# A four-part graph, state-space and expert kernel: the third layernorm's moments moved from VectorE to ScalarE, and the planner's due times replaced

## The chip, the cores and the metric

The kernel runs on one core of one Trainium2 chip. A core has five engines that run their own instruction queues in order and wait for each other by semaphores: TensorE (PE, matrix products; its weight loads are listed as PEld), VectorE (DVE), ScalarE (ACT), GpSimd (POOL) and SyncE (SP, which here issues DMAs only). PE writes its results to PSUM, of which the kernel uses eight banks of 512 floats a partition; DVE and ACT read them from there. The metric is the device time of one execution in microseconds (us), median of several runs.

## The reference

The input is x of 64 graphs x 256 nodes x 256 features and an integer adjacency of 64 x 256 x 256. Two layers are applied, each a graph part and a feed-forward part on a layernorm of x, each added to x:

```python
x = x + _L0_gnn_ref(_layernorm(x), adj, W, a)          # attention over the neighbours
x = x + _L0_ffn_ref(_layernorm(x), W_in, conv_w, ...)  # a state-space (Mamba-2) block, one chunk of 256
x = x + _L1_gnn_ref(_layernorm(x), adj, weight, bias)  # relation products: sum over r of (adj == r) @ x @ weight[r]
x = x + _L1_ffn_ref(_layernorm(x), gate_w, w1, w2, ...) # a mixture of 8 experts, one for each token
```

The layernorm has no weights: `(x - mean) / sqrt(var + eps)`. The third one, before the relation products, is the one whose moments the change concerns.

## The kernel before

There are two passes. The first goes through the 16,384 tokens in 32 groups of two graphs (512 rows, four tiles of 128 rows, indexed j). It does everything up to the choice of the expert, and writes x and the list of the experts' tokens to DRAM. The second (L1187 and after) goes through blocks of tokens of one expert; it gathers rows, does both products and scatters the result. The change is in the first pass only.

A group passes four functions, which add steps to a plan. (Matrix products go through the helper `product`, so the profile gives nearly all of them line 585, and tells them apart by their tiles; the lines below are those of the calls.)

- `attention` (L641): loads x (tile `x`, five buffers) and the adjacency (`adji`), makes the mask `hide`; transposes x to `xT`; takes the first layernorm's moments; products with `wx` to `wh`; attention scores `ev` (three operations over 1024 columns on DVE, L698 to L702, then the exponentials, L705), transposed to `eT`; the attention products `wh,eT` (L728), added to x (L731).
- `scan` (L736): the second layernorm, `xn` and its transpose `xnT`; the step sizes `dt` by a row of some fifteen small DVE operations (L755 to L772); nine input projections `xnT,win` (L777), four of them gates (`gate`) and five convolved: ACT writes `y` (L797), DVE adds three taps (L804), ACT takes the tanh (L810), DVE multiplies (L814, `xh` and `bm`); the decays: PE spreads sums over heads (`sel`, L865), ACT makes `dm` by 32 small relus (L871) and four exponentials (L877).
- `mix` (L893): `bc` from `bm` and `cm`; `xdt` (transposes of `xh`, L914, times `dt`, L919); DVE multiplies each `dm` by `bc` (L929); the products `dm,xdt` (L936, L940); the skip term (L946), the gate (`yg`, L949), the squares (L951), added up on POOL (L954, L956); the out-projection `wf,gate` (L985), the row sums (L992), the factor `r2` and its power on POOL (L996, L998), and the update of x (L1001).
- `relate` (L1006): the third layernorm, split into `xhi` (ACT, through `scaled`, L637) and `xlo` (DVE, L1013); the bias added to x by a POOL DMA with addition (`biased`, L632); the relation products with `adjT` (L1031), `hr` (L1038), the products with `wrel` (L1043), the update of x (L1047); the two DMAs of x to DRAM; and the squares for the router's layernorm (`spreads`, L607), which takes the mean that x carries as column 264 of its row.

The moments of the first three layernorms come from `deviations` (L587): four `bn_stats` and four `bn_aggr` on DVE (L601, L604), one addition (L591), and the power -1/2 on POOL (L593). After every second group `choose` (L1060) finds the expert of 1024 tokens and scatters their slots by eight POOL DMAs (L1123).

The order is not that of the code. `Plan.step` notes each step with its engine, a cost in us, and what it reads and writes; `Plan.record` (L175) then emits all steps by a list schedule over the planner's own costs: of the steps of an engine that are ready it takes the one that can begin first, and of those within 0.05 us of each other the one of the lowest rank. A tile of a tag is made only when its buffers are free and the earlier tiles of that tag have been made. The rank is

```python
step = Step(engine, us, go, self.g, self.TAIL[engine] + late, PACE * self.g + DUE[self.k])
```

with g the group and k the step's number within its group, so `DUE` says how much earlier or later than its group a kind of step is due.

Of the kernel before, what the change touches and what calls it, by code (L numbers as in the profile page):

```python
# [14 lines left out]
ALU = mybir.AluOpType  # L15
# [4 lines left out]
P = 128  # L20
# [5 lines left out]
PE, ACT, DVE, POOL, SP = range(5)  # L26
# [1 line left out]

PACE = 21.50
DUE = [
    -273, -768, -7, 206, -128, -104, -233, 716, 257, 96, 325, 660, -290, -837, -1156, -195, -739,
    -864, 633, -563, -1270, 205, -488, -744, -1044, 252, -389, 419, -601, -43, 36, 132, 68, -155,
    389, 355, -223, -943, 4, 450, -281, 40, -502, 21, 982, 124, 113, 525, -49, 159, 104, 239, 309,
    -615, -359, -749, 426, 428, -391, -391, -326, -1237, -329, -546, -645, -815, -544, -187, -763,
    -683, -372, -601, -139, 290, -500, 172, -270, -586, 121, -388, 994, 458, -317, 125, 17, 277,
    17, 326, -210, -907, 100, -221, -383, -517, 6, 127, 610, 247, -329, -914, -875, -432, -1394,
    67, -309, 571, -93, -248, 110, 916, -78, 172, 34, 14, -122, 417, 67, 66, -569, 10, -1389, 19,
    -452, -183, -558, -20, 528, -605, -550, 387, -39, -686, -315, -111, -118, 33, 835, -632, -115,  # L40
    -192, 1375, -454, -252, 210, 224, 52, -419, -132, 69, 455, 629, 386, -646, 24, 58, 481, -861,
    -1548, -751, -773, 201, 9, 281, -95, 348, 383, 19, -696, -531, -135, -484, -660, 65, 182,
    -280, -194, -875, -1264, -1144, 84, 670, 265, 650, 324, 204, 363, 495, 947, 472, -54, 73, 119,
    -1092, -1060, -382, -668, -147, -96, -599, 715, 36, 69, -120, 106, -707, 33, 160, -559, 353,
    178, -313, 230, -326, -579, 295, 367, -2, -489, -468, -22, 96, -289, 98, -712, -377, 214, 73,
    287, -118, 62, -460, -77, -43, -515, 382, 530, -30, 249, 105, -328, 750, 213, -1302, -231,
    579, -503, -197, -40, 69, -338, -470, -134, -1067, -1028, -435, -550, -387, 677, -404, -211,
    -622, -957, -146, -304, 889, -297, 255, 165, 661, -161, -83, 166, -447, -657, -588, -282,
    -1432, -622, 134, -1056, -541, 582, -9, -25, 592, -45, 94, 540, 638, -1240, -75,
]  # L50


# [16 lines left out]
class AtOnce:  # L69
# [20 lines left out]
    def step(self, engine, us, go, reads, writes, late=0.0):  # L90
        go()
# [9 lines left out]
class Plan:  # L101
# [32 lines left out]
    def step(self, engine, us, go, reads, writes, late=0.0):  # L134
        step = Step(engine, us, go, self.g, self.TAIL[engine] + late, PACE * self.g + DUE[self.k])
        self.k += 1
# [117 lines left out]
def gnn_mamba_rgcn_moe(ctx: ExitStack, tc: tile.TileContext, a: dict, out: bass.AP):  # L254
# [10 lines left out]
    nc = tc.nc  # L265
    x, adj = a["x"], a["adj"]
    B, N, D = x.shape
# [16 lines left out]
    EPS = 1e-5  # L284
# [33 lines left out]
    mhalf = const.tile([P, 8], F32, name="mhalf")  # L318
# [263 lines left out]
    def product(out_, pairs):  # L582

        for i, (lhsT, rhs) in enumerate(pairs):
            nc.tensor.matmul(out_, lhsT=lhsT, rhs=rhs, start=(i == 0), stop=(i == len(pairs) - 1))  # L585

    def deviations(s, src, of):  # L587

        mv, ve, rs = s.tile("mv" + of, [P, 4, 2]), s.tile("ve" + of, [P, 4]), s.tile("rs" + of, [P, 4])
        moments(s, src, mv, 0, of)  # L590
        s.step(DVE, 0.07, lambda: nc.vector.tensor_scalar(  # L591
            ve(), mv()[:, :, 1], EPS, None, ALU.add), [mv], [ve])
        s.step(POOL, 1.0, lambda: nc.gpsimd.tensor_tensor(  # L593
            rs(), ve(), mhalf[:, 0:4], ALU.pow), [ve], [rs])
        return ve, rs

    def moments(s, src, mv, o, of):

        sb = s.tile("st" + of, [P, 4, 6])
        for j in range(4):  # L600
            s.step(DVE, 0.34, lambda j=j: nc.vector.bn_stats(sb()[:, j, :], src()[:, j, 0:D]),  # L601
                   [(src, j)], [(sb, j)])
        for j in range(4):
            s.step(DVE, 0.07, lambda j=j: nc.vector.bn_aggr(mv()[:, o + j, :], sb()[:, j, :]),  # L604
                   [(sb, j)], [(mv, o + j)])

    def spreads(s, src, vr, o):  # L607

        left = s.tile("left", [P, D], BF16)
        for j in range(4):  # L610
            s.step(ACT, 0.58, lambda j=j: nc.scalar.activation(
                left(), src()[:, j, 0:D], AF.Square, bias=src()[:, j, DG - 1 : DG],
                accum_out=vr()[:, o + j : o + j + 1]), [(src, j)], [left, (vr, o + j)])
# [16 lines left out]
    def biased(s, xe, bias):  # L630

        s.step(POOL, 1.4, lambda: nc.gpsimd.dma_start(  # L632
            out=xe()[:, :, 0:DG], in_=bias.unsqueeze(1).to_broadcast([P, 4, DG]),
            accum_op=ALU.add), [], [xe], late=4.5)

    def scaled(s, j, dst, src, rs):
        s.step(ACT, 0.4, lambda: nc.scalar.activation(  # L637
            dst()[:, j, :], src()[:, j, 0:D], AF.Copy, scale=rs()[:, j : j + 1]),
            [(src, j), rs], [(dst, j)])
# [365 lines left out]

    def relate(s, js, o, full, xe, adjT, pair):  # L1006

        ve, rs = deviations(s, xe, "3")

        xhi, xlo = s.tile("xhi", [P, 4, D], F32R), s.tile("xlo", [P, 4, D], F32R)  # L1010
        for j in range(4):
            scaled(s, j, xhi, xe, rs)
            s.step(DVE, 0.4, lambda j=j: nc.vector.scalar_tensor_tensor(  # L1013
                xlo()[:, j, :], xe()[:, j, 0:D], rs()[:, j : j + 1], xhi()[:, j, :].bitcast(F32),
                ALU.mult, ALU.subtract), [(xe, j), rs, (xhi, j)], [(xlo, j)])
        biased(s, xe, brel)
        rels = R if full else 1
        for bi in range(2):
            sums = []
            for r in range(rels):  # L1020
                rel = adjT[bi]
                if full:
                    rel = s.tile("rel", [P, 512], F32R)
                    s.step(DVE, 0.45, lambda r=r, bi=bi, rel=rel: nc.vector.tensor_scalar(
                        rel(), adjT[bi]().bitcast(F32), float(r + 1), None, ALU.is_equal),
                        [adjT[bi]], [rel])
                ps, hr = s.psum(), s.tile("hr", [P, 512], bufs=R if full else 2)

                def related(bi=bi, rel=rel, ps=ps):
                    for d in range(2):  # L1030
                        product(ps()[:, d * N : (d + 1) * N], [  # L1031
                            (part()[:, 2 * bi + k, d * P : (d + 1) * P],
                             rel()[:, k * N : (k + 1) * N])
                            for k in range(2) for part in (xhi, xlo)])

                s.step(PE, 1.05, related, [rel, *((p_, 2 * bi + k) for k in range(2)
                                                  for p_ in (xhi, xlo))], [ps])
                s.step(ACT, 0.47, lambda ps=ps, hr=hr: nc.scalar.copy(hr(), ps()), [ps], [hr])  # L1038
                sums.append(hr)
            weights = pair.get("wrel", wrel)  # L1040
            for h in range(2):
                ps, j = s.psum(), 2 * bi + h
                s.step(PE, 0.9, lambda h=h, ps=ps, sums=sums, weights=weights: product(  # L1043
                    ps()[:, :DG], [
                        (sums[r]()[:, d * N + h * P : d * N + (h + 1) * P], weights[:, r, d, :])
                        for r in range(rels) for d in range(2)]), [*sums], [ps])
                s.step(DVE, 0.35, lambda j=j, ps=ps: nc.vector.tensor_add(  # L1047
                    xe()[:, j, 0:DG], ps()[:, :DG], xe()[:, j, 0:DG]), [ps], [(xe, j)])
        for view in (x3v, outv):
            s.step(SP, 0.1, lambda view=view: nc.sync.dma_start(  # L1050
                out=view[:, js, :], in_=xe()[:, :, 0:D]), [xe], [], late=4.5)

        if o == 0:
            pair["vr"], pair["lg"] = s.tile("vr", [P, 8]), s.tile("lg", [P, 8, E + 1])
        lg = pair["lg"]
        s.step(ACT, 0.22, lambda: nc.scalar.copy(lg()[:, o : o + 4, :], xe()[:, :, D:DG]),
               [xe], [(lg, o)])
        spreads(s, xe, pair["vr"], o)
# [70 lines left out]
    def group(s, g, js, pair, toks, full=False):  # L1129


        s.of(g)
        xe, hide, entries = attention(s, g, js, full)
        ahead = scan(s, g, xe)
        adjT = mix(s, xe, entries, full, *ahead)
        relate(s, js, 4 * (g % 2), full, xe, adjT, pair)
        if g % 2:
            s.of(g + 1, first=False)
            choose(s, toks, pair)
# [244 lines left out]
```

## Time and profile before

| what | value |
|---|---|
| median of 3 runs | 2520.09 us (2518.72 to 2521.66) |
| the profiled execution | 2517.28 us, its span 2515.3 us |
| busy: PE, DVE, ACT, POOL | 2393.0, 1921.1, 1641.2, 838.2 us |
| first matmul of the `dm,xdt` products, group 0 and group 31 | 136.2 and 1762.35 us |
| last `wrel` products of the first pass | from 1796.57 us |
| the chain that ended last reaches back to | 1903.33 us, in the second pass |

The profile lists busy time, which is the union of an engine's instructions; since instructions overlap the start of the next one, a mean duration is longer than the distance between two starts. A row of groups has the line, engine, operation, tiles out and in, shapes and count, then total busy time and mean duration in ns, then the engine's idle time just before them and what ended it. A row of waits reads: who waited, for whom, us in total, times, longest. The chain that ended last lies wholly in the second pass in this profile, so the first pass has to be read by stretches of time and by waits.

### The profile page before, as it was taken

The page shows a single profiled execution, that of the slowest core. Times are in us where ns is not written, and L with a number is a line of the kernel's source. Part 1 is how long each engine was busy: PE and PEld are TensorE (multiplying, and loading weights), DVE is VectorE, ACT ScalarE, POOL GpSimd, SP SyncE. Part 2 cuts the span into 40 slices and gives each one's busy share as a digit, 9 for nine tenths or more (in the row PEclk, how much of TensorE's full clock was granted, in tenths as well). Part 3 has the DMA queues.
Part 4 walks back from the last instruction along what each step waited for, and adds up shares of the span by engine and source line. Part 5 has one row for each costly group of instructions (what it writes and reads, how often), then busy time and mean ns, then how long its engine had stood idle before and what let it go on. Part 6 is the DMA issues. An engine that isn't in the chain of part 4 may idle for free. (4 is left out here: it accounts for less than half of the span.)

```text
span 2515.3 us, 35051 instructions
## 1 busy us (share of the span) xinstructions
PE 2393.0 (95%) x11536; PEld 1667.4 (66%) x11536; DVE 1921.1 (76%) x4776; ACT 1641.2 (65%) x3712; POOL 838.2 (33%) x756
## 2 busy tenths in 40 slices
PE   6799999999999999999999999999559999999998
PEld 4566667766677776777766777666446666666665
DVE  3699999999999999999999999999623344334443
ACT  0688788888888888888888888888312222332232
POOL 0122343343333433334343343432532222222222
PEclk7899999999999999999999999999779999999999
DMA  2302222223222232222332222312264333333333
GB/s 79 100 12 64 63 54 62 64 67 75 54 62 54 71 79 56 54 62 70 68 67 53 62 68 57 81 37 54 52 194 122 122 107 116 120 115 117 110 124 74
DMA packets 171135, 196.53 MB, mean 78 GB/s; under 512 B 24919, under 2 KB 155807, under 8 KB 170800
## 3 DMA queue, kind: packets, MB, share of 16 engines
q1 hardware_dynamic: 122144, 133.11, 16.9%
q0 software_dynamic: 47104, 59.14, 12.7%
q8 instruction: 97, 1.59, 0.3%
q10 hardware_dynamic: 1680, 1.79, 0.2%
q14 instruction: 110, 0.90, 0.1%
HBM read 109.05 MB, written 47.06 MB: 62 GB/s over the span
## 5 line engine op out<-in xcount | busy, mean ns | idle before, releaser
L585 PE MATMUL ps<-xnT,win 128*128 128x512 f32 x1152 | 546.1, 600 | 3.9 <-ACT xnT L627 3.9
L804 DVE SCALAR_TENSOR_TENSOR y<-ps,cw,y 128x510 f32<-128x510 f32 (+2 forms) x480 | 349.6, 738 | 6.1 <-ACT y L797 2.8
L871 ACT ACTIVATE dm<-ps,cs 128x256 f32<-128x256 f32 (+1 forms) x1024 | 334.1, 475 | 11.5 <-PE ps L585 11.4
L593 POOL TENSOR_TENSOR rs<-ve,mhalf 128x4 f32<-128x4 f32 x96 | 155.1, 1616 | 508.2 <-DVE ve L591 490.3
L1298 PE MATMUL ps<-xnT,w 128*128 128x512 f32 (+1 forms) x768 | 318.0, 573 | 3.9 <-DVEq L1346 3.9
L1308 PE MATMUL ps<-w,hid 128*128 128x256 f32 x1440 | 318.7, 379 | 0.0
L585 PEld LDWEIGHTS ps<-xnT,win 128*128 128x128 f32 x1152 | 203.1, 190 | 166.1 <-issue 153.7
L1308 PEld LDWEIGHTS ps<-w,hid 128*128 128x128 f32 x1440 | 271.7, 190 | 44.9 <-issue 10.0
L1298 PEld LDWEIGHTS ps<-xnT,w 128*128 128x128 f32 x768 | 148.1, 193 | 161.2 <-issue 147.9
L585 PE MATMUL ps<-wf,gate 128*128 128x265 f32 x1024 | 251.9, 389 | 1.0 <-DVE gate L949 0.6
L1302 ACT ACTIVATE hid<-ps,b 128x512 f32<-128x512 f32 (+1 forms) x192 | 126.8, 661 | 183.1 <-PE ps L1298 183.1
L1313 DVE TENSOR_TENSOR yv<-ps,b 128x256 f32<-128x256 f32 x90 | 38.2, 425 | 254.4 <-PE ps L1308 254.4
L585 PEld LDWEIGHTS ps<-wf,gate 128*128 128x128 f32 x1024 | 192.8, 191 | 49.4 <-issue 11.3
L929 DVE TENSOR_TENSOR dm<-dm,bc 128x1536 f32<-128x1536 f32 x128 | 224.1, 1754 | 0.8 <-ACT dm L877 0.2
L1329 POOL DMA_INDIRECT out_dram<-yf,place x90 | 89.1, 990 | 372.3 <-DVE yf L1328 366.9
L877 ACT ACTIVATE dm<-dm 128x1536 f32<-128x1536 f32 x128 | 198.9, 1558 | 0.0
L1123 POOL DMA_INDIRECT slots<-meta,sl x128 | 133.5, 1043 | 191.0 <-DVE sl L1120 150.8
L1314 ACT ACTIVATE yv<-yv,meta 128x256 f32<-128x256 f32 x90 | 45.8, 508 | 201.5 <-DVE yv L1313 201.5
L936 PE MATMUL ps<-dm,xdt 128*64 128x256 f32 x1024 | 168.6, 396 | 4.7 <-DVE dm L929 4.4
L601 DVE BATCH_NORM_STATS2 st<-x 128x6 f32<-128x256 f32 x384 | 155.1, 416 | 6.1 <-DMA x<-in_x_dram 4.5
L954 POOL TENSOR_TENSOR xh<-xh 128x512 f32<-128x512 f32 x64 | 107.5, 1680 | 132.2 <-ACT xh L951 132.1
L585 PE MATMUL ps<-wh,eT 128*128 128x273 f32 x512 | 143.5, 405 | 0.0
(244 smaller groups left out, 4913.3 us busy)
## 6 DMA issues: line engine op xcount, KB each, us to landing
w<-in_L_ffn_w_dram SPq DMA_DIRECT2D x52, 1024.0 KB, 5.6
x<-blin POOLq DMA_DIRECT2D x32, 530.0 KB, 7.3
x<-brel POOLq DMA_DIRECT2D x32, 530.0 KB, 7.0
adji<-in_adj_dram SPq DMA_DIRECT2D x32, 512.0 KB, 3.9
x<-in_x_dram SPq DMA_DIRECT2D x32, 512.0 KB, 4.9
x3d<-x SPq DMA_DIRECT2D x32, 512.0 KB, 3.1
out_dram<-x SPq DMA_DIRECT2D x32, 512.0 KB, 4.1
cm<-bm SPq DMA_DIRECT2D x32, 128.0 KB, 2.2
```

The lines of the kernel that those rows point to most:

```text
L585: nc.tensor.matmul(out_, lhsT=lhsT, rhs=rhs, start=(i == 0), stop=(i == len(pairs) - 1))
L593: s.step(POOL, 1.0, lambda: nc.gpsimd.tensor_tensor(rs(), ve(), mhalf[:, 0:4], ALU.pow), [ve], [rs])
L601: s.step(DVE, 0.34, lambda j=j: nc.vector.bn_stats(sb()[:, j, :], src()[:, j, 0:D]), [(src, j)], [(sb, j)])
L804: nc.vector.scalar_tensor_tensor(y3[:, :, d:], p3[:, :, : N - d], cw[:, c, k : k + 1], y3[:, :, d:], ALU.mult, ALU.add,)
L871: nc.scalar.activation(dm()[:, q, bi, o : o + n], ps()[:, t0 + N - n : t0 + N], AF.Relu, bias=cs()[:, j, h : h + 1], scale=-1.0,)
L877: s.step(ACT, 1.38, lambda: nc.scalar.activation(dm(), dm(), AF.Exp, scale=-1.0), [], [dm])
L929: s.step(DVE, 1.67, lambda dm=dm: nc.vector.tensor_mul(dm(), dm(), bc().unsqueeze(1).to_broadcast([P, 2, 2, N + P])), [bc], [dm])
L936: nc.tensor.matmul(o, lhsT=xdt()[:, 2 * bi, h * 64 : (h + 1) * 64], rhs=dm()[:, q, bi, 0:N], start=True, stop=False,)
L1123: s.step(POOL, 1.1, lambda j=j: apart("slots", nc.gpsimd.indirect_dma_start(out=slots, out_offset=bass.IndirectOffsetOnAxis(ap=sl()[:, j : ...
L1298: nc.tensor.matmul(ps[:, :n], lhsT=w1[:, k, f * P : (f + 1) * P], rhs=xnT[:, k, :], start=(k == 0), stop=(k == 1),)
L1302: nc.scalar.activation(hid[:, f, :], ps[:, :n], AF.Relu, bias=self.b1[i % 2][:, f : f + 1])
L1308: nc.tensor.matmul(ps[:, :D], lhsT=hid[:, f, j * P : (j + 1) * P], rhs=w2[:, f, :], start=(f == 0), stop=(f == NFT - 1),)
```

## The change

Two things change. In `relate` the third layernorm's moments no longer come from `deviations`; four ACT squares take the deviations from the mean in x's row and sum them (`spreads`, with the same single buffer `left` as the router's squares), DVE turns the sums into variance plus eps, POOL takes the power. And the table of due times is replaced: all of the offsets become 0, and `PACE` becomes 13.60. The list has a number for each step of a group, in the order in which the functions add them.

```diff
-PACE = 21.50
+PACE = 13.60
 DUE = [
-    -273, -768, -7, 206, -128, -104, -233, 716, 257, 96, 325, 660, -290, -837, -1156, -195, -739,
...
-    -1432, -622, 134, -1056, -541, 582, -9, -25, 592, -45, 94, 540, 638, -1240, -75,
+    0, 0, 0, 0, 0, 0, 0, 0, 0, 0, 0, 0, 0, 0, 0, 0, 0, 0, 0, 0, 0, 0, 0, 0, 0, 0, 0, 0, 0, 0, 0,
...
 ]
@@
     def relate(s, js, o, full, xe, adjT, pair):
 
-        ve, rs = deviations(s, xe, "3")
+        vr, rs = s.tile("vr3", [P, 4]), s.tile("rs3", [P, 4])
+        spreads(s, xe, vr, 0)
+        s.step(DVE, 0.07, lambda: nc.vector.tensor_scalar(
+            vr(), vr(), 1.0 / D, EPS, ALU.mult, ALU.add), [], [vr])
+        s.step(POOL, 1.0, lambda: nc.gpsimd.tensor_tensor(
+            rs(), vr(), mhalf[:, 0:4], ALU.pow), [vr], [rs])
```

## The prediction

> **What bounds the kernel now.** I read the page first, then the busy time by stretches, then the waits of single engines, then rows by shape. The page:
>
> ```profile
> span 2515.3 us, 35051 instructions
> ...
> PE   6799999999999999999999999999559999999998
> ...
> DVE  3699999999999999999999999999623344334443
> ACT  0688788888888888888888888888312222332232
> ```
>
> Slices 3 to 28 are the first pass (32 groups of four 128-row tiles), the rest is the experts' pass. The change touches the first pass alone; the experts' pass I leave at its time. The first pass by stretches (columns: PE, weight loads, DVE, ACT, POOL busy, granted clock, DMA):
>
> ```profile
> 125.00:600.00 475.00, 469.64 (x2495) 329.16 (x2494) 451.16 (x1024) 402.62 (x942) 161.36 (x133) 1.00 0.25 55
> 600.00:1100.00 500.00, 497.42 (x2665) 349.47 (x2664) 477.21 (x1135) 426.04 (x1000) 197.48 (x164) 1.00 0.29 66
> 1100.00:1700.00 600.00, 595.97 (x3164) 419.02 (x3163) 572.71 (x1362) 504.96 (x1184) 229.65 (x189) 1.00 0.27 61
> ```
>
> PE is busy 1563 of 1575 us, 99.2%, at full clock; DVE 95.3%, ACT 84.7%. The busy PE really streams: in the timeline the projections' matmuls follow each other every 0.43 us. PE waits, from 125 to 1700 us:
>
> ```profile
> PE ps L585 <- ACT xnT L627: 3.4, 15, 0.2
> PE ps L622 <- ACT xn L637: 3.1, 15, 0.2
> ```
>
> So PE sets the pace, and only 12 us of the pass are left to win. The first `dm,xdt` matmul of group 0 starts at 136.2 us, that of the last group at 1762.35: 1626 us for 31 steps, 52.5 us a group. Work a group: PE 52, DVE 50, ACT 44.5. All three are near full, so the order in which they are fed decides.
>
> **Part 1, the third layernorm's moments.** The rows:
>
> ```profile
> L593 POOL TENSOR_TENSOR rs<-ve,mhalf 128x4 f32<-128x4 f32 x96 | 155.1, 1616 | 508.2 <-DVE ve L591 490.3 <-DVE mv L604 11.6 <-ACT wh L675 6.1
> L601 DVE BATCH_NORM_STATS2 st<-x 128x6 f32<-128x256 f32 x384 | 155.1, 416 | 6.1 <-DMA x<-in_x_dram 4.5
> ...
> L604 DVE BATCH_NORM_AGGREGATE mv<-st 128x2 f32<-128x6 f32 x384 | 65.1, 173 | 1.6
> ```
>
> Four of each leave DVE per group. Durations overlap the next start, so I use the distance of starts: 0.33 and 0.09 us. 4 x 0.42 = 1.7 us, over 32 groups 54 us of DVE. The small `ve` operation and the POOL power (1.6 us) stay, one for one. ACT gets four squares with the sum read out; the router's four squares are the same shape. At the end of the pass they stand back to back:
>
> ```profile
> 1805.59 0.51 ACT L611 ACTIVATE left<-x 128x256 bf16<-128x256 f32 x1
> 1806.01 0.19 ACT L611 ACTIVATION_READ_ACCUMULATOR left<-x 128x1 f32 x1
> 1806.22 0.51 ACT L611 ACTIVATE left<-x 128x256 bf16<-128x256 f32 x1
> ```
>
> 0.63 us from start to start, 2.5 us a group, 80 us of ACT in all: DVE 48, ACT 47 a group, both under PE's 52. If PE stayed covered, this part would be worth nothing, with all of PE's idle time (12 us) as the most it could give. Two orders are new: both uses of squares share one `left` buffer, so group g+1's moments stand behind group g's router squares; and on ACT they stand ahead of `xhi`. Neither matters at 52 us a group: from the first of the moments' squares to x complete it is some 16 us in the walk below. The small DVE operation on the variance now waits for ACT's squares; behind it on DVE stand the next group's x updates, its statistics and `xlo`, for which POOL's power and PE's relation products wait.
>
> **Part 2, the due times.** All offsets become 0, so of steps that could start together the older group's goes first, whatever PACE is. I read the order of the changed program's instructions on each engine. It repeats every two groups from group 2 to 27. Counting PE's own work (its instructions by their distances in the trace) from a group's first `dm,xdt` matmul: before, its last `wrel` product comes 101 us later, two groups on, and the next group's attention products stand 15 us ahead of it. After, `wrel` ends 28 to 31 us behind it, and the next group's attention stands 14 us behind it for an even group, 4 us ahead for an odd one. Group g is nearly finished before g+1 may begin its input projections. What hid the latency between engines before (other groups' work) is gone. I walk one even and one odd group through the new order, with starts' distances from the trace (us: convolution tap 0.66, `dm` product 1.68, `x` updates 0.34 to 0.41, ACT copies 0.48, one PE projection 1.71) and about 0.25 us from PE to a reader, 0.1 elsewhere.
>
> Even group g, from its first `dm,xdt` matmul. `dm,xdt` 5.2. DVE's four `yg` are done at 7.8, so PE's out-projection (16 matmuls, 7.2) ends at 13.8, the row sums at 14.6. `r2` and the power (1.2): 16.3. The four L1001 updates: 18.0. PE does g+1's attention only now, 15.9 to 19.6; DVE's updates and stats for it end at 21.7. POOL: third layernorm's power to 21.7, the next group's second to 23.4. ACT: squares 16.9 to 19.7, `xhi` to 23.5, `xn` to 25.1. PE: relation products, half of g+1's transposes, `wrel` to 30.3, other half 30.7. The bias DMA is issued at `xlo`'s end, 24.0, and takes 7.0 (its row): x is complete at 32.5. On ACT the first router square stands ahead of the second `xnT` copy, so this waits for x: 32.7. Only here g+1's projections run. From here to the last `dm` exponential ACT has 29.2 us of own work (32 relus at 0.305 = 9.8, 4 exponentials 5.5, 5 `y` 3.3, 5 tanh 2.7, 4 gates 2.0, `ev` and `exp` 3.0, the rest 2.9) and waits 4.2 for taps and projections: 66.1. The ACT distances are from rows like
>
> ```profile
> 1015.55 5.10 ACT L871 ACTIVATE dm<-ps,cs 128x256 f32<-128x256 f32 x16 [0.68 <-PE ps L585]
> 1020.43 1.60 ACT L877 ACTIVATE dm<-dm 128x1536 f32<-128x1536 f32 x1
> ```
>
> Then the `dm` products and the last `xdt`: the next group's first `dm,xdt` matmul at 70.7.
>
> Odd group. Attention of g+1 is done, `rs` of its second layernorm at 11.5, `xn` at 13.2; but its transposes stand behind the out-projection (8.3 to 15.5) and row sums: 17.2; `xnT` 18.0. L1001 updates done at 19.6, squares at 21.9; the power waits on POOL behind another group's `wh` product and power until 24.0; `xhi` 25.7, `xlo` 26.2, bias lands 33.3, x complete 34.8. ACT from 18.0: 34.5 of own work, 8.3 of waits (1.5 for that power, 2.8 for x, the rest taps): 60.8. Next first `dm,xdt` matmul: 62.9.
>
> **The clock.** While PE idles in front of the `xh` transposes (10 us and more in both walks) its clock falls. The end of the pass shows it (here the clock is the last column but two):
>
> ```profile
> 1766.00:1770.00 4.00, 1.88 (x20) 1.46 (x16) 4.00 (x5) 2.34 (x4) 1.21 (x2) 1.00 0.00 0
> 1770.00:1772.00 2.00, 1.26 (x8) 0.90 (x9) 2.00 (x5) 0.00 (x0) 1.02 (x1) 0.50 0.00 0
> ...
> 1776.00:1778.00 2.00, 2.00 (x9) 1.61 (x8) 2.00 (x8) 0.26 (x1) 1.85 (x2) 0.79 0.00 0
> ```
>
> After 1.10 and 1.75 us of idling with 1.0 of work between, half clock from 1770.7 to about 1777, 6.3 us. The Trainium skill, "TensorE: Matmul & The Clock Gate", Part 1, says half rate after an idle window of about 3.4 us and full rate after one busy window of the same length. It speaks against this change, and more mildly than the row: 3.4 us cold would add about 1.1 to the even and 0.5 to the odd group, the row's 6.3 us adds 2.2 and 1.0 (transposes 1.7 us longer, then part of the attention products; the rest is behind DVE).
>
> **Sum.** From group 0 to 31 there are 15 even-type steps (groups 2 to 30) and 16 odd-type ones (0, 1 and the odd). With the row's clock 15 x 72.9 + 16 x 63.9 = 2116 us against 1626: +490; by the rule +465; without a clock effect +441. The drain is shorter, the last group having the engines to itself: from its first `dm,xdt` matmul to the last `wrel` it takes 38 us now, some 28 in the walk: -10. The start I leave. Profiled execution 2517.3 (2 us more than its span), median of the runs 2520.1: 2520 + 480 = 3000 by the row, 2975 by the rule, 2951 without. I take 2970, a little under the row's, since some of the cold time lies beside DVE work. A check: at the end of the pass, with no other group to hide behind, the row sums end at 1782.5 and the relation products begin at 1792.4, 9.9 us; my walk has 9.0 for the same stretch. A step of 4 us a group in the walk is 124 us: with it as the error 2850 to 3095.
>
> **Rivals.** (1) The walk's waits overlap more than I see, and the pace is DVE's 48 us of work plus its waits for powers, row sums and exponents, some 9: 57 us a group, 2520 + 31 x 4.5 - 10 = 2650. For it: DVE has work of the other group in the list; against it: the list is in order, and each wait holds all behind it. Chance 0.09. (2) PE stays covered, the groups' order makes no difference: 2510 to 2525. For it only PE's small waits now; against it the order read above. 0.02. (3) Faster: the shorter drain (-10) and the moments' 1.7 us off DVE, while the steps stay at 52.5: 2505. It decides if the new order costs under 10/31 = 0.3 us a group. The planner does fill an idle engine with younger work; but single buffers for `wh`, `ev`, `xnT` bar it from going further. 0.05.
>
> **Numbers.** Much slower, as walked: 0.84, own range 2720 to 3100. All cases together: 2680 to 3100 holds 0.8 of that and a little of (1). Faster 0.05, within 0.2% (about what a measurement of this kernel can tell) 0.02, slower 0.93.
>
> **What would show it.** PE busy about 75% in the first pass, with waits of 3 us and more for DVE at the `xh` transposes (L914) and `dm,xdt` (L936); granted clock under 0.9 there; steps between first `dm,xdt` matmuls alternating near 73 and 64; ACT waiting for x at the router squares; BATCH_NORM rows at x256, the square's at x256. Wrong if PE is over 90% busy, or if the steps are equal: then the latencies do overlap, and my walk of a strict order has put waits in a row that run side by side.

## The result and the profile after

| | before | after |
|---|---|---|
| median (lowest to highest), us | 2520.41 (2518.72 to 2521.66) | 2911.76 (2909.87 to 2912.98) |
| profiled execution, its span, us | 2517.28, 2515.3 | 2912.98, 2911.2 |
| first `dm,xdt` matmul of group 0 and of group 31, us | 136.2, 1762.3 | 138.7, 2166.8 |
| mean of the 31 steps between groups, us | 52.46 | 65.42 |

After over before is 1.1553, 95% interval 1.1533 to 1.1573: the changed kernel is 15.5% slower. Forecast were 2970 us (2680 to 3100) and "slower" with 0.93.

The place of the 395.9 us between the two spans: the 31 steps from the first group's `dm,xdt` to the last one's take 2028.1 us instead of 1626.1 (+402.0), they begin 2.5 later, the drain from there to the end of the last `wrel` product takes 31.8 instead of 38.3 (-6.5), and all behind it 712.6 instead of 714.6 (-2.1). The whole loss is in the steady part of the first pass.

In the changed kernel lines from 43 to 1000 have numbers smaller by 7 than in the kernel before, lines from 1007 on smaller by 2: the `xh` transposes are L907, `dm,xdt` L929 and L933. Its page:

```profile
span 2911.2 us, 35216 instructions
...
PE   6888888878888888878888888878882999999998
...
DVE  3787778877877777777877777887863334343433
ACT  0867777777677776777676776777651332322322
...
PEclk7889999989999999988999999998985999999999
```

TensorE's row, all nines in the first pass before, is now at 8 nearly all through it, and its clock dips too. The same three stretches as before (PE, weight loads, DVE, ACT, POOL busy, granted clock, DMA):

```profile
125.00:600.00 475.00, 403.68 (x2027) 280.61 (x2027) 375.46 (x789) 349.50 (x831) 120.75 (x113) 0.91 0.22 50
600.00:1100.00 500.00, 430.91 (x2168) 298.57 (x2166) 391.64 (x864) 363.15 (x864) 145.37 (x136) 0.93 0.24 54
1100.00:1700.00 600.00, 508.41 (x2548) 352.79 (x2547) 470.27 (x1020) 434.98 (x1032) 159.92 (x151) 0.92 0.23 51
```

TensorE is busy 1343 of 1575 us, 85.3% (99.2% before), VectorE 78.6% (95.3%), ScalarE 72.9% (84.7%). No engine is full: the first pass now waits. TensorE's waits from 125 to 1700 us:

```profile
PE ps L907 <- DVE xh L807: 93.9, 24, 5.4
PE ps L578 <- ACT dm L864: 70.8, 57, 3.1
PE ps L907 <- ACT dm L864: 15.0, 13, 1.4
```

Before, the longest entry of this list was 3.4 us. The `xh` transposes wait once in nearly every group (24 times in 24 groups' time, 3.9 us each) for the last product of VectorE's convolution. In the second row TensorE waits for ScalarE's small relus to be done with a bank, ahead of the sums over heads (`sel`) and of small products of `choose`. The moments' rows:

```profile
L594 DVE BATCH_NORM_STATS2 st<-x 128x6 f32<-128x256 f32 x256 | 100.4, 412 | 4.8 <-DMA x<-in_x_dram 4.7
...
L604 ACT ACTIVATION_READ_ACCUMULATOR left<-x 128x1 f32 x256 | 48.0, 187 | 0.0
...
L597 DVE BATCH_NORM_AGGREGATE mv<-st 128x2 f32<-128x6 f32 x256 | 29.1, 158 | 0.1
```

384 statistics have become 256, 128 squares 256, as the change says. The steps alternate: from an even group to the next one they take 72.1 to 75.1 us (67.8 and 69.1 at the end of the pass), from an odd one 58.5, with 62.8, 60.7 and 58.3 at the two ends.

### The profile page after: what moved, and what is told of

Read it like the earlier page. It is cut to its first block, busy times and chain, and to the rows that moved or that the text cites. A ratio compares the mean times of both kernels' runs of the same rounds, so it can differ in the third digit from the quotient of the medians.

```text
span 2911.2 us, 35216 instructions
## 1 busy us (share of the span) xinstructions
PE 2497.4 (86%) x11536; PEld 1724.9 (59%) x11536; DVE 1946.7 (67%) x4520; ACT 1728.7 (59%) x3968; POOL 775.9 (27%) x756
## 5 line engine op out<-in xcount | busy, mean ns | idle before, releaser
L578 PE MATMUL ps<-xnT,win 128*128 128x512 f32 x1152 | 515.2, 594 | 0.0
L797 DVE SCALAR_TENSOR_TENSOR y<-ps,cw,y 128x506 f32<-128x506 f32 (+2 forms) x480 | 345.1, 737 | 33.4 <-ACT y L790 32.2
L578 PEld LDWEIGHTS ps<-xnT,win 128*128 128x128 f32 x1152 | 213.4, 190 | 228.6 <-issue 208.1
L947 POOL TENSOR_TENSOR xh<-xh 128x512 f32<-128x512 f32 x64 | 90.8, 1433 | 766.2 <-ACT xh L944 766.0
L1121 POOL DMA_INDIRECT slots<-meta,sl x128 | 183.8, 1436 | 325.9 <-DVE xdt L912 254.2
L907 PE MATMUL ps<-ident,xh 128*128 128x128 f32 x512 | 124.6, 421 | 148.8 <-DVE xh L807 128.8
L907 PEld LDWEIGHTS ps<-ident,xh 128*128 128x128 f32 x512 | 98.7, 220 | 206.9 <-DVE xh L807 142.0
L944 ACT ACTIVATE xh<-gate 128x512 f32<-128x512 f32 x128 | 80.0, 630 | 210.1 <-DVE gate L942 210.1
L929 PE MATMUL ps<-dm,xdt 128*64 128x256 f32 x1024 | 183.3, 399 | 0.6 <-DVE xh L939 0.5
```

The costliest lines, as they stand in the source:

```text
L797: nc.vector.scalar_tensor_tensor(y3[:, :, d:], p3[:, :, : N - d], cw[:, c, k : k + 1], y3[:, :, d:], ALU.mult, ALU.add,)
L907: nc.tensor.transpose(ps()[:, c * P : (c + 1) * P], xh()[:, c, j * P : (j + 1) * P], ident)
L929: nc.tensor.matmul(o, lhsT=xdt()[:, 2 * bi, h * 64 : (h + 1) * 64], rhs=dm()[:, q, bi, 0:N], start=True, stop=False,)
L1121: s.step(POOL, 1.1, lambda j=j: apart("slots", nc.gpsimd.indirect_dma_start(out=slots, out_offset=bass.IndirectOffsetOnAxis(ap=sl()[:, j : ...
```

## The experiments

All times are medians; a ratio is to the kernel before, run beside it. That kernel itself took 2526.5 us in the first group of experiments and 2524.8 in the third (e8 to e11), both on one chip, and 2555.1 in the second (e5 to e7), on another chip, from which there is no trace of it. So across chips ratios are compared; where times would say something else, both are given.

**e1, the moments alone.** With them on ScalarE, and the old table:

```diff
 PACE = 21.50
-... 295, 367, -2, -489, -468, -22, 96, -289, 98, -712, ...   # third layernorm: statistics, aggregates, variance, power
+... 295, 367, -2, -489, 98, -712, ...                        # squares, variance, power
```

> Only the third layernorm's moments go to ScalarE. The due times stay those of the kernel before: the four squares take the four that the statistics had, the aggregates' four are dropped, all others keep theirs. A (my sum: where PE is covered the moments are worth nothing): 2505 to 2530 us, steps between groups near 52.5. B (the due times fit the old list of steps, and dropping four and moving four to another engine spoils the order): 2600 to 2650; the depth stays (by PE's own work a group's last wrel product comes 92 to 104 us after its first dm,xdt matmul, as before), so a loss would come from the fine order, which now repeats every four groups. C (the moments carry the loss of the change): about 2900.

2705.95 us, ratio 1.0713 (1.0695 to 1.0731). All three expectations missed, B by the least. The steps' mean is 58.47 us, in a pattern of four groups (55.2, 60.2, 54.6, 63.6 to 66.9 us). TensorE is busy 1483 of 1575 us, 94.2%; its waits from 125 to 1700 us begin

```profile
PE ps L929 <- DVE dm L922: 26.4, 18, 3.9
PE ps L578 <- DVE xlo L1011: 17.5, 17, 1.6
```

The wait for `xlo` is the moments' own chain (squares, variance, power, `xhi`, `xlo`), but the longest is for `dm`, which the moments don't touch. So the depth of the pipeline stayed (in the trace a group's last `wrel` product ends 110 to 123 us behind its first `dm,xdt` matmul, 105 to 106 before), and 180 us went all the same. Whether the moments or the order cost them, e5 and e11 tell.

**e2, the due times alone.** The kernel before, statistics on VectorE, with

```diff
-PACE = 21.50
+PACE = 13.60
-DUE = [-273, -768, -7, ...]
+DUE = [0] * 300
```

> Only the due times: all zero, while the third layernorm keeps its statistics on VectorE. A (my sum: the moments add nothing to the due times' loss): 2895 to 2930 us. B (with zero due times the order follows from which step can start first, so the moments change it too): in this order three groups of four have the next group's attention products 5 to 12 us ahead of their own first dm,xdt matmul, where the changed kernel has it so in one of two; with the steps measured there, 24 of 58.5 and 7 of 72.6 make 1912 us against 2028, that is 2795. C (the due times carry nothing): 2520.

2830.07 us, ratio 1.1202 (1.1184 to 1.1221). A is refuted: without the moved moments the zeros cost 304 us, not all of the 390. B's mechanism holds, its size is 35 us short: steps near 56 and 58 us, two of four, and 69 to 70, the other two; it had counted three short ones. The two parts alone make 180 and 304 us, 484 together, and both at once 386 (e10): they are not terms that add up.

**e3, three due times by hand.** On the changed kernel:

```diff
-PACE = 13.60
-DUE = [0] * 300
+PACE = 20.00
+DUE = [-50] * 53 + [-30] * 111 + [0] * 123   # attention, scan, the rest
```

> The changed kernel with three due times put in by hand in place of the zeros: attention steps -50, scan steps -30, all others 0, PACE 20. By PE's own work the next group's attention products now stand 28 to 82 us ahead of a group's first dm,xdt matmul, its projections begin up to 38 us ahead of it. A (the loss is that of a pipeline one group deep): more than half of the 391 us come back, 2620 to 2730 us, PE over 92% busy in the first pass. B (the loss is that of the fine order within a group): 2850 to 2950.

2765.25 us, ratio 1.0945 (1.0926 to 1.0963). Between A and B: 38% of the loss comes back, not over half. The steps are uneven, from 17.1 to 99.0 us, and TensorE is busy 1444 of 1575 us, 91.7%. Going ahead with the next group is worth some 148 us by the ratios; where it goes ahead but out of rhythm, the rest stays lost.

**e4, the bias taken off x.** On the changed kernel, in `relate`; the output lacks that bias:

```diff
-        biased(s, xe, brel)
+        s.step(POOL, 1.4, lambda: nc.gpsimd.dma_start(
+            out=scrap, in_=brel.unsqueeze(1).to_broadcast([P, 4, DG]),
+            accum_op=ALU.add), [], [xe], late=4.5)
```

> The changed kernel with the bias transfer of the relation part added to a tile that nobody reads, in place of x: the output lacks that bias, and x no longer waits for the transfer; the order of all instructions is unchanged. A (the steps are one chain in which x complete comes late): the four updates of x can follow the wrel products one by one, 0.6 to 0.9 us earlier in each group, 18 to 28 us in all: 2884 to 2894 us. B (a loose chain, ScalarE or the taps set the step): 2908 to 2914. C (all of VectorE's idling for the transfer, 2.4 us in even and 0.7 us in odd groups, lies on the path): 2865.

2910.65 us, ratio 1.1529 (1.1510 to 1.1548), against 1.1530 for the changed kernel itself (e10): no difference, B. The wait is gone from VectorE's list. From 125 to 1700 us the changed kernel has there

```profile
DVE x L1045 <- DMA x<-brel: 37.6, 24, 3.2
```

and the experiment, for the same update, only this:

```profile
DVE x L1050 <- PE ps L578: 13.6, 33, 0.5
```

x is complete 0.8 us earlier in the odd group 17, the router's squares begin 0.85 us earlier, and at ScalarE's next `gate` all is as before (35.05 us after the group's first `dm,xdt` matmul in both): it waits for its projection, and TensorE was busy with projections all along. In the even group 18 ScalarE was busy with the mask until 32.4 us anyway. x complete is not on the path that sets the step.

**e5, six due times set anew.** As e1, but

```diff
-... 295, 367, -2, -489, 98, -712, ...
+... 42, 196, -1000, 124, -37, 1000, ...
```

The six numbers, and those of e6, come from a random search that kept what brought the end of the planner's own list schedule forward.

> The moments on ScalarE with the due times of the kernel before (as in the first experiment), but the six of the third layernorm's own steps set anew (squares 42, 196, -1000, 124, the small VectorE operation -37, the power 1000); the other 281 stay. By PE's own work the order is now that of the kernel before to within 1 to 2 us in every group (next attention 15 ahead, projections from 12.5 to 50, last wrel 102 behind), except that the relation products begin at 74 to 75 us instead of 61 to 66. A (the 180 us of the first experiment are due times that no longer fit, the moments cost nothing where PE is covered): 2515 to 2560, PE over 98% busy. B (the chain of squares, VectorE, power, xhi, xlo ahead of the relation products costs the time itself): 2650 to 2710.

2562.81 us beside 2555.13, ratio 1.0037 (1.0022 to 1.0051): A in kind, its range missed by 3 us on the chip where the kernel before is slower too. Of e1's 7.1%, 6.8 points were due times that no longer fitted; moved moments and a remaining misfit together cost 0.4%. Why the kernel before took 30 us more on this chip is not known. Held against 2526.5 us on the other chip, e5 would be 1.4% slower: even so four fifths of e1's loss were due times. The stretches and TensorE's waits:

```profile
125.00:600.00 475.00, 464.95 (x2470) 325.71 (x2471) 440.26 (x945) 414.69 (x992) 149.23 (x134) 1.00 0.26 55
600.00:1100.00 500.00, 487.87 (x2592) 344.16 (x2591) 462.67 (x1037) 438.20 (x1051) 171.33 (x156) 1.00 0.28 62
1100.00:1700.00 600.00, 590.55 (x3168) 416.96 (x3168) 560.56 (x1248) 529.23 (x1276) 206.87 (x192) 1.00 0.28 62
```

```profile
PE ps L578 <- DVE xlo L1011: 9.6, 13, 0.8
PE ps L615 <- DMA x<-in_x_dram: 8.2, 8, 1.8
```

TensorE is back at 98.0% (99.2% before) and at full clock. VectorE has lost 38 us against the kernel before in these stretches (1463.5 for 1501.1), ScalarE gained 48 (1382.1 for 1333.6), and nothing comes of it: TensorE sets the pace. The moments' chain still shows, as 9.6 us of waiting for `xlo`.

**e6, a whole table for the new list.** The changed kernel with 287 due times and PACE 9.12 from the same search.

```diff
-PACE = 13.60
-DUE = [0, 0, 0, ...]
+PACE = 9.12
+DUE = [12975, 528, 3870, 8430, 4314, ...]
```

> The changed kernel with all 287 due times and PACE searched for the new list of steps. By PE's own work the next group's attention products stand 38 us ahead of a group's first dm,xdt matmul, its projections begin 11 to 12 us ahead, the last wrel product comes 85 us behind; all groups alike. A (moments are worth nothing, a fitted table is worth the 390 us): 2505 to 2545, PE over 98% busy; with its 12 us of idle in the kernel before, no more than 12 us under it. B (moments cost at least part of what the first experiment lost): 2600 or more.

2570.81 us, ratio 1.0060 (1.0043 to 1.0076): A in kind, above its 2545 us in time on a chip where the kernel before took 2555. A quite different order (next attention 38 us ahead instead of 15) gets back all but 0.6 of the 15.3%, by the ratios. Neither version beats the kernel before; with 12 us of idle TensorE in it there was little to win.

**e7 and e9, TensorE kept warm; e10, the changed kernel beside e9.** In `mix`, where the `xh` transposes of the first tile are issued, `fill` being 40 where the next group is odd, and 20 (e7) or 12 (e9) where it is even:

```diff
                 for c in range(NCT):
+                    if c == 3:
+                        for _ in range(fill):
+                            nc.tensor.transpose(ps()[:, 3 * P :], xh()[:, 0, 0:P], ident)
                     nc.tensor.transpose(
```

> The changed kernel with idle TensorE kept at work ahead of the last 13 xh transposes: 40 more transposes (4.4 us) into the part of the bank that the fourth transpose writes next, where the next group is odd, 20 where it is even. No other instruction moves. A (the cold clock is on the path: the 13 transposes take 3.0 us instead of 1.4, and stand ahead of dm,xdt): 1.2 to 1.6 us a group, 2860 to 2877. B (VectorE's xdt and dm products set the start of dm,xdt anyway): 2905 to 2915. C (the additional transposes end later than the last xh and push it): over 2920.

2905.85 us, ratio 1.1372 (1.1350 to 1.1394). By its time this is B; by its ratio, held against 1.1530 for the changed kernel (e10), it would be 40 us better, which is A. I go by the time, because the trace shows nothing slower on this chip and no gain of A's size: the projections' matmuls take 594 ns in the mean in both kernels, all behind the first pass takes 711.7 us (712.6 in the changed kernel), and the mean step is 65.20 us (65.42), not 1.2 us less. e9 repeated the experiment with the changed kernel beside it.

> The changed kernel with 40 more transposes ahead of the last 13 xh transposes where the next group is odd, as before, and only 12 where it is even (20 ended 0.5 us later than the last xh). To be held against the changed kernel run beside it. A (the cold clock is on the path by what 20 took away, 0.5 us in every second group): 5 to 12 us less than the changed kernel. B (not on the path at all): within 3 us of it. C (by the clock term of my sum): 25 to 49 us less.

> The changed kernel itself, beside the two above on one chip: 2905 to 2920 us by all theories.

e10: 2911.05 us, ratio 1.1530 (1.1511 to 1.1550). e9: 2925.66 us, 1.1585 (1.1566 to 1.1605), 14.6 us more: none of the three expectations. The transposes did become faster; in the changed kernel, ahead of group 18, and in e7:

```profile
1312.63 3.03 PE L907 MATMUL ps<-ident,xh 128*128 128x128 f32 x13 [2.65 <-DVE xh L807]
1315.60 1.13 PE L929 MATMUL ps<-dm,xdt 128*64 128x256 f32 x4
```

```profile
1309.92 1.58 PE L910 MATMUL ps<-ident,xh 128*128 128x128 f32 x13
```

But a step from an even group, 73.0 us in the middle of the pass, stays (73.2 in e7), since VectorE's `dm` and `xdt` products stand in a row there; a step from an odd group, 58.5 us, falls to 57.9 and 57.8, by 0.7 us x 16 = 11 us.

That is not all that the cold clock costs. Most even steps of the changed kernel have one of two lengths, about 72.3 or 73.5 us, and what sets them apart is whether half clock ends before or within the next group's attention products, behind which TensorE goes straight on to `dm,xdt` (groups 18 and 10):

```profile
1383.90 3.85 PE L578 MATMUL ps<-wh,eT 128*128 128x273 f32 x16
856.34 4.60 PE L578 MATMUL ps<-wh,eT 128*128 128x273 f32 x16
```

With the transposes of `ev` ahead of them, about 1 us is lost in seven of the fifteen even steps, 7 us. So I estimate the cold clock's cost at 11 + 7 = 18 us. e7 does not get them all back: in four of its even steps TensorE waits 1.0 us for POOL's sums, and in the step from group 20, behind the 40 additional ones, the last 13 transposes begin 0.9 us after the product that they wait for.

In e9 the even steps became longer, 75.2 us. There TensorE waits ahead of the row sums, and its clock falls two us later, inside the next group's attention (group 18; clock in the last column but two):

```profile
1339.00:1341.00 2.00, 1.00 (x5) 0.52 (x3) 0.00 (x0) 0.00 (x0) 1.91 (x2) 1.00 0.00 0
1341.00:1343.00 2.00, 1.96 (x16) 1.75 (x16) 0.16 (x1) 0.37 (x1) 0.62 (x1) 1.00 0.00 0
1343.00:1345.00 2.00, 1.76 (x5) 1.37 (x5) 1.54 (x4) 1.68 (x5) 0.43 (x1) 0.53 0.00 0
1345.00:1347.00 2.00, 2.00 (x7) 1.51 (x6) 0.66 (x2) 1.43 (x6) 0.00 (x0) 0.61 0.04 8
```

```profile
1341.05 1.05 PE L578 MATMUL ps<-tri,xh 128*128 128x1 f32 x8 [1.04 <-POOL xh L952]
1343.27 5.55 PE L578 MATMUL ps<-wh,eT 128*128 128x273 f32 x16 [0.24 <-ACT eT L716]
```

In e10 the same two rows read

```profile
1330.25 0.98 PE L578 MATMUL ps<-tri,xh 128*128 128x1 f32 x8
1332.40 3.95 PE L578 MATMUL ps<-wh,eT 128*128 128x273 f32 x16 [0.24 <-ACT eT L716]
```

1.6 us of the lengthening are the attention products at half clock; 1.55 us stand ahead of them (row sums 17.66 us after the group's first `dm,xdt` matmul, 16.11 in e10), for the most part the wait for POOL, which has the eight scatters of `choose` ahead of the sums of squares (they end at 13.7 us in e9, 12.1 in e10). Why the scatters were slower there isn't settled.

**e8, two buffers.** The changed kernel, zeros kept:

```diff
-        wh = s.tile("wh", [P, 4, WX])
+        wh = s.tile("wh", [P, 4, WX], bufs=2)
-        ev = s.tile("ev", [P, 4, N])
+        ev = s.tile("ev", [P, 4, N], bufs=2)
...   # and wh's second buffer at the two places where its tag is set up
```

> The changed kernel, zero due times kept, with two buffers in place of one for wh and for ev. By PE's own work the next group's attention products now stand 9 to 10 us ahead of a group's first dm,xdt matmul in every group (14 behind and 4 ahead before); its projections still begin 15 to 18 us behind it, the last wrel product comes 30 to 39 us behind. A (single buffers bar the attention of the next group from going ahead, and with it ahead every step is like the short one of the changed kernel): 58 to 60 us a step, 2690 to 2750 us. B (what counts is that the projections start late, attention's place does not matter): 2880 to 2915. C (a pipeline that keeps TensorE covered): under 2600.

2752.4 us, ratio 1.0897 (1.0874 to 1.0919): 159 of the 386 us come back, A but for 2 us. With attention ahead in every group the steps from even groups fall from 73.0 to 63.2 us in the middle of the pass, those from odd ones stay (58.5 to 58.0). The even steps do not become quite like the odd ones, as A had it, but the single buffers do bar the way for a planner that serves the oldest group first.

**e11, one due time of 291.** The kernel before, with

```diff
-... 96, -289, 98, -712, ...     # the variance's small operation: 98
+... 96, -289, 1000, -712, ...
```

> The kernel before, statistics on VectorE and all, with one of its 291 due times changed: that of the third layernorm's small VectorE operation on the variance, from 98 to 1000, so that it goes behind whatever else can start. The order of the instructions is then another in every group (next attention 3 to 45 us ahead, projections from 26 ahead to 30 behind). A (the table's worth is in a finely fitted order, one entry can spoil it as the moved moments did): 2590 to 2720. B (single entries matter little): 2515 to 2540.

2662.38 us, ratio 1.0549 (1.0532 to 1.0567): A. One number, no instruction more or less on any engine, costs 138 us. TensorE is busy 1490 of 1575 us; the steps go from 25.0 to 101.1 us, and TensorE now waits where the kernel before hardly did:

```profile
PE ps L585 <- ACT hr L1038: 18.6, 15, 2.8
PE ps L936 <- DVE dm L929: 16.7, 11, 2.9
```

So e1's loss needs no price of the moments: another place in the list for one small step of the same layernorm does as much.

## Why the prediction was right, and where not

**What bounds the kernel, and the direction: right.** TensorE set the pace, 52 us of it a group, and the order kept it fed. The order that I read from the changed program (next attention 14 us behind for even groups, 4 ahead for odd ones) is what took the cover away: e8 puts attention ahead again and gets 41% back, e3 38%, e5 and e6 with a fitted table all but 0.4 and 0.6% of the time, by the ratios. What keeps e8's steps at 60 us instead of 52.5 no run takes apart; that e8's projections still begin late is a reading of its order, not shown as the cause.

**Part 1, the moments: the step that failed.** "If PE stayed covered, this part would be worth nothing" holds to 0.4% (e5, 1.4% against the other chip), but it stays covered only if the table is fitted to the new list. With the old one e1 lost 180 us: squares on ScalarE shift what is ready when, and every later choice of the planner with it. "Neither matters" of the two new orders was read off the totals; the totals (VectorE 48, ScalarE 47, TensorE 52 us a group) could not tell it, and e11 shows how little it takes. Nor was the due times' part the whole loss: alone it is 304 of 386 us. My total did not suffer from this, because the walk was made in the order of both parts together.

**Part 2, the even step: right in size, by terms that cancel.** Forecast 72.9, measured 72.4 in the mean of 15. From the first `dm,xdt` matmul of group 18 (at 1315.60; the ends of the out-projection and of `wrel` by the distance of starts, as in the walk):

| us after it | forecast | measured |
|---|---|---|
| fourth `yg` | 7.8 | 10.0 |
| out-projection ends, row sums end | 13.8, 14.6 | 16.0, 17.0 |
| L1001 updates end (L994 after) | 18.0 | 20.1 |
| moments' squares, `xhi`, `xn` end | 19.7, 23.5, 25.1 | 21.4, 25.2, 26.8 |
| `wrel` ends | 30.3 | 32.0 |
| x complete | 32.5 | 33.4 |
| last `dm` exponential ends | 66.1 | 66.9 |
| next first `dm,xdt` matmul, before the clock's 2.2 | 70.7 | 72.1 |

Two us were missing at the start. VectorE's timeline there has no gap:

```profile
1317.12 0.68 DVE L912 TENSOR_TENSOR xdt<-ps,dt 128x512 f32<-128x512 f32 x1
1317.72 1.75 DVE L922 TENSOR_TENSOR dm<-dm,bc 128x1536 f32<-128x1536 f32 x1
1319.39 0.74 DVE L939 SCALAR_TENSOR_TENSOR xh<-xh,dch,ps 128x512 f32<-128x512 f32 x1
1320.05 1.22 DVE L691 SCALAR_TENSOR_TENSOR ev<-ev 128x1024 f32<-128x1024 f32 x1
1321.18 0.74 DVE L939 SCALAR_TENSOR_TENSOR xh<-xh,dch,ps 128x512 f32<-128x512 f32 x1
```

The last `xdt` (0.60 to the next start) and the score operation of group 19 (1.13) stand among this group's skips and gates; with them VectorE's own work from the first `dm,xdt` matmul to the fourth `yg` is 10 us. POOL's sum of squares ends at the same time as the out-projection, 15.9, behind eight scatters (the last ends at 12.0), which my walk did not name. At x complete the lag is down to 0.9 us, since the bias takes 5.9 us from issue to landing where I took 7.0 from its row. The clock's 2.2, of which this step shows nothing over the attention products and the longer even steps about 1, then stood in for the 0.9 and for 0.5 to 1.4 us that the end of the step takes longer than in the walk.

**The odd step: mis-sized.** Forecast 63.9, measured 58.5 (58.9 in the mean of 16). This is the whole error: my sum by the row, from the profiled execution's 2517.3, was 2997; 16 x 5.0 less for the odd steps, 15 x 0.5 less for the even ones, 3.5 more for the drain (-6.5 for -10), 2.5 more for the start and 2 less behind it make 2913, the measured execution. Of the 84 us the choice of 2970 had taken 30 off beforehand. In the odd group 17 the marks are right up to the moments' squares (21.9 forecast, 21.8 measured). Then: the power on POOL ends at 23.2, not 24.0; the bias lands at 31.4, not 33.3; the last exponential ends at 58.8, not 60.8. The "2.8 for x" among ScalarE's waits is 0.8 in the trace, and e4 shows that even this is not on the path. The next first `dm,xdt` matmul stands 0.3 us ahead of the end of that exponential, where I had it 2.1 behind: it begins when VectorE's third `xdt` product ends (58.45), which stands behind the last `xh` (55.5), not behind the last `dm`. The clock's share, 0.6 to 0.7 (e7, e9) where I added 1.0, lies within that. 2.0 + 2.4 + 1.0 are the 5.4 us between 63.9 and 58.5.

**The clock: priced too high.** The trace has more cold time than the rule of the Trainium skill ("TensorE: Matmul & The Clock Gate", Part 1: half rate after an idle window, full rate after a busy one of about 3.4 us) would give one idle wait. Ahead of group 18 half clock lasts from 1308.4 to 1318.7 us: between 1304.9 and 1312.6 TensorE works only 1.2 us, in two pieces. From the restart of the `xh` transposes to full clock it takes 2.8 to 6.0 us in the groups from 2 to 27 (4.7 at group 17, 6.0 at group 18), so that both the page's figure and the 6.3 us that I took lie in or near what is seen. What I had wrong is the price. The row made it +49 us, the rule +24; my estimate from the traces is 18, near the rule's, because VectorE stood beside most of the cold time. How much of it is paid is in part luck: with the same order of instructions, half clock reaches into the attention products in one even step and not in the next.

**The signs that I named.** TensorE busy 75%: it is 85.3%; its 52 us of work in a step of 65.4 are 79.5%, and most of the rest is matmuls at half clock, which take longer and count as busy all the while (13 transposes 3.03 us for 1.58 in e7). Clock under 0.9: 0.91 to 0.93. Waits of 3 us and more at the `xh` transposes: right (3.9 in the mean), at `dm,xdt` wrong. Steps alternating: right. ScalarE waiting for x at the router's squares: in odd groups, by 0.8 us, and off the path. Counts of 256: right.

**The rivals.** Overlap (2650) lost: VectorE's pace was no bound, it is 78.6% busy. No difference, and faster, fell with the first 386 us; "a shorter drain" is real, 6.5 us, and drowned.

## What to carry to other kernels

Where three engines are some 85% busy and more and a written-out or planned order keeps them so, the order is what one owns: a list of priorities fitted to one set of steps is worth nothing certain for another set, and moving a few cheap steps to another engine (e1) or one priority (e11) can cost 5 to 7%, with not a single us of work added where it counts. Read the order of the changed program and walk it in both parities, with every engine's foreign work in its place (the next group's score operation, the scatters on POOL), and test each wait in such a walk for another that ends at the same time before it is given a price. After such an edit fit the list again before the edit is judged: six numbers turned 7.1% into 0.4% (by the ratios).

## What the runs showed of the hardware

A short wait can be followed by a loss of clock some us later, in the middle of dense work, but need not be. In e9 a wait of 1.0 us ahead of the row sums (1.3 in group 2), TensorE otherwise busy or idle by 0.5 us at a time, is followed one to two us later by 3.4 us at half clock in every even step from group 2 to 26; twelve of the fifteen even steps have a length of 75.1 us and more. The changed kernel has the same wait in group 16, and the attention products behind it run at full clock:

```profile
1199.24 1.05 PE L578 MATMUL ps<-tri,xh 128*128 128x1 f32 x8 [1.02 <-POOL xh L949]
1201.47 3.95 PE L578 MATMUL ps<-wh,eT 128*128 128x273 f32 x16 [0.24 <-ACT eT L716]
```

So do those of e7 in the groups 8, 12, 20 and 26, which have this wait too. The wait alone does not decide; what else does is not settled. In e9 keeping the engine warm at one place came with cold time at a dearer one, and 40 and 12 additional transposes in turn left the kernel 14.6 us slower.
